# First group of a masked-attention stack on one core: fills, order of keys and queries, mask copies and a fourth buffer for adj

## The chip, the cores and the metric

The kernel runs on one core of a Trainium2 chip. The metric is the device time in microseconds (us). The engines are TensorE (PE), VectorE (DVE), ScalarE (ACT), GpSimd (POOL) and SyncE (SP), which here issues nearly all DMAs, in order, from one queue.

## The reference

`x` has 3327 rows of 256, `adj` is a 3327 x 3327 matrix of 0 and 1. Four layers follow each other, each with a residual and a layer norm; layer 3 holds three attention steps in a row. All use the same `adj` as a mask. The first group, with which this case deals, belongs to layer 0:

```python
def _L0_gnn_ref(features, adj, Wq, Wk):
    Qn = _cos_normalize(features @ Wq.T)      # x / max(|x|, 1e-4)
    Kn = _cos_normalize(features @ Wk.T)
    raw_att = Kn @ Qn.T
    att = softmax(where(adj > 0, raw_att, -9e15), axis=1)
    prop_fea = att @ features
    adj_mask = (sum(adj, axis=1) > 0)[:, None]
    prop_fea = adj_mask * prop_fea + (1.0 - adj_mask) * features
    return 0.5 * prop_fea + 0.5 * features

x = _layernorm(x + _L0_gnn_ref(x, adj, Wq, Wk))     # layer 0
x = _layernorm(x + _L1_gnn_ref(x, adj, W, a))       # layer 1: leaky_relu(s_i + d_j), softmax, elu
x = _layernorm(x + _L2_gnn_ref(x, adj, ...))        # layer 2: q k^T / sqrt(d), softmax, elu
x = _layernorm(x + _L3_gnn_ref(x, adj, ...))        # layer 3: three steps like layer 1
```

## The kernel before

**Tiling.** The rows are padded to 26 tiles of 128 (`NT`). The rows whose result is computed are taken in groups of 512 (`b`, `NB` = 7, the last with 256). A step is one pair of a group `b` and a tile `j` of 128 neighbours: a product `ps` (L493) of 128 neighbours by the 512 rows of the group, an exponential on ScalarE (`ex`, L506), a multiplication with the mask on VectorE (`e`, L507), and four products `po` (L1331, 128x257) with tile `j` of `x`, added up over the 26 steps. The 257th column of `x` is one, so that the sum of the weights comes along. Groups 1 to 5 of layer 0 use other products (L780) and stand outside the change. There are 6 such passes over 7 groups.

**Order.** The main loop makes the weights `e` two to three steps ahead of their `po` (`LA` = 2, function `make`). The program up to step 3 is written out by hand (`tc.manual_schedule`, closed with `start.__exit__` at `s == 3`); after that a planner with its own costs sets the order on each engine, so that moving one instruction can change the order further on. Every engine, and SP's queue too, works its list in order: an instruction that waits holds all behind it.

**The start.** `ones` is set by VectorE; a few products of `ones` with itself (L80) have no use for the result. `count` and `part` are used for the identity matrix `ident` (L94, L96), which later turns tiles on TensorE. Then, for group 0: `queries0(0)` computes the 512 rows of `pk` (L354) in two banks, their squares on ScalarE (L369), the inverse lengths `rk` on VectorE, the scaled rows `kr` (L389 on VectorE, L391 on ScalarE), turns them on TensorE (`pkT`, L395) and copies them to half 1 of `FT[0]` (L396). `keys0(0)` computes the other side turned at once: `pq` (L317), its square (L324), a copy to half 0 of `FT[0]` (L336), the sums of squares `pn` (L330), and from them `qss` and `rq` on VectorE (L338 and the lines 137 to 160). The bank pool `ps_b` has three banks.

**adj.** For each group, `adj` comes in 13 loads of two tiles, 512 KB each (`load_adj`, L425), into tiles with the tag `stage`, of which there are three. `take_adj` makes a byte mask of each; for the first four loads of group 0 that is one `tensor_scalar` (L434), on GpSimd for the first two and on VectorE for the next two; later ones take two passes on ScalarE (L437, L438). `add_adj` adds the two halves into a count (L447, L451); `sum_adj` turns the count (`af`, `pasum`, L462 and L466). A `stage` tile is free again when both have read it. Tiles with other names (`turned`, `p4`, `x4`, `o4`, `x2`) use the same tag in later layers.

**SP's queue at the start:** weights, `xT` of groups 0 and 1, adj (0,0), x tiles 0 to 3, adj (0,2) and (0,4), x tiles 4 to 7, `xT` of group 2, x tile 8, adj (0,6), and so on, with (b, j) for group and first tile.

The order of the parts before the loop is this line:

```python
for part in (k0, q0, k0, q0, q0, k0, q0, k0, q0, q1):
    next(part, None)
```

Of the kernel before, what the change touches and what calls it, by code (L numbers as in the profile page):

```python
# [19 lines left out]
P = 128  # L20
# [13 lines left out]
def gnn_stack(ctx: ExitStack, tc: tile.TileContext, a: dict, N: int, out: bass.AP):  # L34
# [41 lines left out]
    nc.vector.memset(ones, 1.0)  # L76

    turned = bank("turned")
    for _ in range(4):
        nc.tensor.matmul(turned[:, :P], ones, ones, start=True, stop=True)  # L80

    count = const.tile([P, P], F32, name="count")
    n = 8
    for k in range(n):
        nc.vector.memset(count[:, k : k + 1], k + 1.0)
    while n < P:
# [1 line left out]
            count[:, n : 2 * n], count[:, :n], float(n), None, ALU.add  # L88
        )
        n *= 2  # L90
    part = const.tile([P, P], F32, name="part")
    nc.vector.memset(part, 1.0 / (4 * P))
    for k in range(4):
        nc.tensor.matmul(turned[:, :P], count, part, start=(k == 0), stop=(k == 3))  # L94
# [216 lines left out]
    def keys0(g):  # L311

        wd, n = bw(g), len(tiles_of(g))
        xT = xTs[g]
        pm = bank("pq")
        for h in range(2):
            nc.tensor.matmul(  # L317
                pm[:, :wd], w["qk"][:, h, :H], xT[:, h, :wd], start=(h == 0), stop=(h == 1)
            )
            if g == 1 and h == 0:  # L320
                yield
        yield
        sq = work.tile([P, CH], F32, tag="u", name="qsq", bufs=2)
        nc.scalar.activation(sq[:, :wd], pm[:, :wd], AF.Square)  # L324
        if g > 0:
            nc.scalar.copy(FT[g][:, 0, :wd], pm[:, :wd])
        yield
        pn = bank("pn0")
        for k in range(n):
            nc.tensor.matmul(  # L330
                pn[:, k : k + 1], sq[:, k * P : (k + 1) * P], ones[:, :1], start=True, stop=True
            )
        yield
        v = cols.tile([P, 4], F32, tag="qss", name="qss")
        if g == 0:
            nc.scalar.copy(FT[g][:, 0, :wd], pm[:, :wd])  # L336
            yield
            nc.vector.tensor_scalar(v[:, :n], pn[:, :n], COS_EPS * COS_EPS, None, ALU.max)  # L338
            rsqrt(rq[:, 4 * g : 4 * g + n], v[:, :n], n)
        else:  # L340
            nc.scalar.copy(v[:, :n], pn[:, :n])
            lengths(rq[:, 4 * g : 4 * g + n], v[:, :n], n)

    def queries0(g):

        wd, n = bw(g), len(tiles_of(g))
        xT = xTs[g]
        ss = cols.tile([P, 4], F32, tag="kss", name="kss")
        kr = work.tile([P, 4, H], F32, tag="kr", name="kr", bufs=1)
        banks = [bank("pk") for _ in range(2 if g == 0 else 1)]  # L350
        for k in range(n):
            pk = banks[k // 2 if g == 0 else 0][:, k * H : (k + 1) * H]
            for h in range(2):
                nc.tensor.matmul(  # L354
                    pk,
                    xT[:, h, k * P : (k + 1) * P],
                    w["qk"][:, h, H:],
                    start=(h == 0),
                    stop=(h == 1),
                )  # L360
        if g > 0:
            nc.scalar.copy(kr.rearrange("p k n -> p (k n)")[:, :wd], banks[0][:, :wd])
            yield
        src = [
            banks[k // 2][:, k * H : (k + 1) * H] if g == 0 else kr[:, k, :] for k in range(n)
        ]
        for k in range(n):
            jk = work.tile([P, H], F32, tag="sq0", name="sq", bufs=1)
            nc.scalar.activation(jk, src[k], AF.Square, accum_out=ss[:, k : k + 1])  # L369
        yield  # L370
        rk = cols.tile([P, 4], F32, tag="rk", name="rk")
        if g == 0:
            lengths(rk[:, :n], ss[:, :n], n)
        else:
            lengths(rk[:, :n], ss[:, :n], n, nc.gpsimd, "prs")
            for _ in range(4 if g == 1 else 7):
                yield

            r2 = cols.tile([P, 4], F32, tag="rk2", name="rk2")
            nc.vector.scalar_tensor_tensor(  # L380
                r2[:, :n], gate[0][:, :n], 0.0, rk[:, :n], ALU.is_ge, ALU.mult
            )
            rk = r2
        yield
        for k in range(n):
            if g > 0 and k == 2:
                yield
            if g == 0 and k >= 2:
                nc.vector.tensor_scalar(kr[:, k, :], src[k], rk[:, k : k + 1], None, ALU.mult)  # L389
            else:  # L390
                nc.scalar.mul(kr[:, k, :], src[k], rk[:, k : k + 1])  # L391
        yield
        pt = bank("pkT")
        for k in range(n):
            nc.tensor.transpose(pt[:, k * P : (k + 1) * P], kr[:, k, :], ident)  # L395
        nc.scalar.copy(FT[g][:, 1, :wd], pt[:, :wd])  # L396
# [20 lines left out]
    def load_adj():  # L417

        if not adj_order:
            return  # L420
        b, j = adj_order.popleft()
        wd = bw(b)
        st = work.tile([P, 2 * CH], I32, tag="stage", name="stage", bufs=3)
        src = a["adj_a"][b] if wd == CH else a["adj_z"]
        nc.sync.dma_start(st[:, : 2 * wd], src[:, j * wd : (j + 2) * wd])  # L425
        stages[b, j] = st

    def take_adj(b, j):

        wd = bw(b)  # L430
        st = stages[b, j][:, : 2 * wd]
        if b == 0 and j < 8:
            eng = nc.gpsimd if j < 4 else nc.vector
            eng.tensor_scalar(mask(b, j, 2), st, 0, None, ALU.is_gt)  # L434
        else:
            t_ = work.tile([P, 2 * CH], BF16, tag="a", name="pos", bufs=3)
            nc.scalar.activation(t_[:, : 2 * wd], st, AF.Relu)  # L437
            nc.scalar.activation(mask(b, j, 2), t_[:, : 2 * wd], AF.Sign)  # L438
# [45 lines left out]
    def weights0(b, j):  # L484
        wd = bw(b)
        if j % 2 == 0:
            take_adj(b, j)
            load_adj()
        soon = (b, j) in ((0, 0), (0, 2))
        if j % 2 == 0 and not soon:  # L490
            add_adj(b, j)
        ps = bank("ps")
        nc.tensor.matmul(  # L493
            ps[:, :wd],
            FT[j // 4][:, 0, (j % 4) * P : (j % 4 + 1) * P],
            FT[b][:, 1, :wd],
            start=True,
            stop=True,
        )
        t_ = work.tile([P, CH], F32, tag="a", name="ex", bufs=3)  # L500
        e = work.tile([P, CH], F32, tag="e", name="e", bufs=5)

        n = 2 if (b, j) == (0, 0) else 1
        for h in range(n):
            c = slice(h * wd // n, (h + 1) * wd // n)
            nc.scalar.activation(t_[:, c], ps[:, c], AF.Exp, scale=rq[:, j : j + 1])  # L506
            nc.vector.scalar_tensor_tensor(  # L507
                e[:, c], t_[:, c], 0.0, mask(b, j)[:, c], ALU.add, ALU.mult
            )
        if soon:  # L510
            add_adj(b, j)
        return e
# [315 lines left out]
    def turn(x4, n, out, steps=3):  # L828

        half = "p k (n t) -> p t k n"
        pl = work.tile([P, 4, 2, D], U16, tag="x4k", name="planes", bufs=2)
        for t in range(2):
            nc.scalar.copy(pl[:, :n, t, :], x4[:, :n, :].bitcast(U16).rearrange(half, t=2)[:, t])
        yield
        tr = work.tile([P, 16, P], U16, tag="stage", name="turned", bufs=3)
        nc.sync.dma_start_transpose(
            out=tr[:, : 4 * n, :], in_=pl[:, :n].rearrange("p k t n -> p (k t n)")
        )  # L840
        for _ in range(steps):
            yield
        trv = tr[:, : 4 * n, :].rearrange("p (k t h) i -> p t k h i", t=2, h=2)
        for t in range(2):
            nc.vector.tensor_copy(out(t), trv[:, t])  # L845
        yield
# [19 lines left out]
    def finish(L, b, pos):  # L866
# [74 lines left out]
                if k % 2:  # L941
                    yield
        else:
            p4 = work.tile([P, 4, D], F32, tag="stage", name="p4", bufs=3)
            if L.key == "2":
                z = joined(pos, b, p4)
                nc.vector.tensor_scalar(z, z, TINY, None, ALU.max)
# [9 lines left out]
                    nc.vector.reciprocal(ri, ri)  # L957
                    nc.scalar.mul(p4[:, k, :], pos[k][:, :D], ri)  # L958
            if L.key in x_d:
                x4 = work.tile([P, 4, D], F32, tag="stage", name="x4", bufs=3)  # L960
                xr = [x4[:, k, :] for k in range(4)]
                for k, t in enumerate(ts_):
                    nc.sync.dma_start(xr[k], x_d[L.key][t])
            else:
                xr = [cur[t][:, :D] for t in ts_]
# [67 lines left out]
        if not L.hidden:  # L1033
# [3 lines left out]
            rsqrt(r[:, :n], v[:, :n], n)  # L1037
            yield
            if L.key in ("1", "3c"):
                o4 = work.tile([P, 4, D], F32, tag="stage", name="o4", bufs=3)  # L1040
                dsts = [o4[:, k, :] for k in range(n)]
            else:
                dsts = [nxt[t][:, :D] for t in ts_]
# [72 lines left out]

    def fetch_last():

        x2 = work.tile([P, 2, D], F32, tag="stage", name="x2", bufs=3)
        for k, t in enumerate(tiles_of(NB - 1)):  # L1120
            nc.sync.dma_start(x2[:, k, :], x_d["3c"][t])
        xm = work.tile([P, 2, D], F32, tag="acc", name="xm", bufs=2)
# [121 lines left out]
    load_adj()  # L1244
    load_x(0)
    load_adj()
    masks[0] = new_mask(0)
    k0, q0, q1 = queries0(0), keys0(0), keys0(1)
    for part in (k0, q0, k0, q0, q0, k0, q0, k0, q0, q1):
        next(part, None)  # L1250
    make(0)
    next(q1)
# [202 lines left out]
```

## Time and profile before

| | |
|---|---|
| median of 3 runs | 2375.55 us (2374.44 to 2375.63) |
| profiled execution | 2374.08 us |
| its span, first to last instruction | 2372.3 us |
| TensorE busy | 2346.0 us, 99% |
| VectorE busy | 1598.1 us, 67% |
| ScalarE busy | 1223.5 us, 52% |
| GpSimd busy | 43.5 us, 2% |
| mean granted TensorE clock | 0.997 |
| moved by DMA | 214.66 MB |

Times in the timeline count from the first instruction. A busy row of TensorE is no proof of work at its peak, since the ends of products are modelled; the granted clock (1.00 is full) is given apart. The DMA share is the mean busy share of the 16 DMA engines. In the lists of waits a line says which engine waited at which line for whom, the total in us, how often, and the longest. In the timeline an idle time before an instruction and what ended it stand in brackets.

### The profile page before, as it was taken

How to read it: one execution, taken by the hardware profiler on the slowest of the kernel's cores; microseconds unless marked ns; L12 is line 12 of the kernel's file. 1: busy time of each engine (PE TensorE's matmuls, PEld its weight loads, DVE VectorE, ACT ScalarE, POOL GpSimd, SP SyncE). 2: the span in 40 equal slices, each digit the busy share in tenths (PEclk: the TensorE clock that was granted, in tenths of full speed). 3: DMA queues.
4: the chain of work that ended last, by engine and by line, in shares of the span. 5: the costliest groups of instructions: out<-in, count | busy, mean ns of one | idle time of the engine just before them, and what ended most of it. 6: DMA issues, size and time to landing. Idle time of an engine off the chain costs nothing.

```text
span 2372.3 us, 33071 instructions
## 1 busy us (share of the span) xinstructions
PE 2346.0 (99%) x11957; PEld 1914.3 (81%) x11957; DVE 1598.1 (67%) x4243; ACT 1223.5 (52%) x1959; POOL 43.5 (2%) x158
## 2 busy tenths in 40 slices
PE   9999999999999999999999999999999999999997
PEld 6788887888888777667667798888888888888886
DVE  6789999866666657567567585556656555655665
ACT  4667777765555422222222255555655555655554
POOL 1000001000000000000000000000000000000000
PEclk9999999999999999999999999999999999999999
DMA  7555555423232322212212221211211111122120
GB/s 256 188 182 181 185 187 191 161 83 83 74 87 53 105 56 87 78 53 88 74 49 73 80 87 48 75 52 26 76 47 43 43 59 51 44 98 69 61 66 23
DMA packets 147288, 214.66 MB, mean 90 GB/s; under 512 B 76093, under 2 KB 101172, under 8 KB 142516
## 3 DMA queue, kind: packets, MB, share of 16 engines
q1 hardware_dynamic: 146852, 212.28, 29.0%
q8 instruction: 94, 1.54, 0.3%
q14 instruction: 70, 0.57, 0.1%
q10 hardware_dynamic: 272, 0.26, 0.0%
HBM read 167.53 MB, written 28.19 MB: 83 GB/s over the span
## 4 chain that ended last, share of the span: by engine, by line
PE 89%; DVE 5%; DMA 3%; ACT 2%; issue 1%; POOL 0%; SPq 0%; DVEq 0%; ACTq 0%
PE po L1331 47%; PE po L780 18%; PE ps L564 12%; PE ps L493 4%; PE pproj L989 3%; DMA stage<-in_adj_a 1%; PE pv L1075 1%; DMA turned<-planes 1%; DVE e L507 1%; PE pgq L523 1%; PE po L1316 1%; DVE acc L451 1%; ACT re L658 1%; DVE ejunk L592 0%; DVE v L669 0%
## 5 line engine op out<-in xcount | busy, mean ns | idle before, releaser
L1331 PE MATMUL po<-v,e 128*128 128x257 f32 x5616 | 1251.9, 381 | 2.1 <-ACT p L958 1.4
L1331 PEld LDWEIGHTS po<-v,e 128*128 128x128 f32 x5616 | 1062.0, 190 | 169.5 <-ACT p L958 9.4
L658 ACT ACTIVATE re<-u,nrh,th 128x512 f32<-128x512 f32 (+1 forms) x728 | 555.4, 780 | 476.9 <-DVE e L669 472.5
L669 DVE SCALAR_TENSOR_TENSOR e<-re,rh,mask 128x512 f32<-128x512 f32 (+1 forms) x702 | 501.2, 719 | 377.1 <-PE po L1331 348.8
L564 PE MATMUL ps<-gT,ft 128*128 128x512 f32 (+1 forms) x728 | 307.4, 563 | 0.0
L572 ACT ACTIVATE ex<-ps,off 128x512 f32<-128x512 f32 (+1 forms) x182 | 119.1, 656 | 356.8 <-PE ps L564 356.1
L780 PE MATMUL po<-tsums,ssum 128*128 128x128 f32 (+1 forms) x1794 | 250.1, 275 | 0.4 <-DVE ssum L730 0.3
L479 DVE SCALAR_TENSOR_TENSOR e<-ex,mask 128x512 f32<-128x512 f32 (+1 forms) x182 | 118.4, 651 | 162.8 <-ACT ex L572 161.9
L780 PEld LDWEIGHTS po<-tsums,ssum 128*128 128x128 f32 x1794 | 224.7, 192 | 1.7 <-DVE ssum L730 1.0
L564 PEld LDWEIGHTS ps<-gT,ft 128*128 128x128 f32 x728 | 132.1, 190 | 114.5 <-issue 111.7
L780 PEld LDWEIGHTS po<-v,e 128*128 128x128 f32 x1196 | 169.4, 191 | 67.4 <-issue 54.5
L780 PE MATMUL po<-v,e 128*128 128x129 f32 x1196 | 182.6, 275 | 0.0
L506 ACT ACTIVATE ex<-ps,rq 128x512 f32<-128x512 f32 (+1 forms) x183 | 119.1, 652 | 117.9 <-PE ps L493 107.9
L493 PE MATMUL ps<-ft,ft 128*128 128x512 f32 (+1 forms) x312 | 142.5, 561 | 0.0
L507 DVE SCALAR_TENSOR_TENSOR e<-ex,mask 128x512 f32<-128x512 f32 (+1 forms) x183 | 117.1, 647 | 31.6 <-ACT ex L506 27.3
L451 DVE CUSTOM_DVE_ANT_0 acc<-acc,stage 128x1024 uint16<-128x1024 uint16 (+1 forms) x168 | 108.4, 645 | 18.3 <-DMA stage<-in_adj_a 13.9
L780 PE MATMUL po<-tsums,e 128*128 128x128 f32 x598 | 92.3, 275 | 0.1
L780 PE MATMUL po<-v,ssum 128*128 128x128 f32 x598 | 92.3, 275 | 0.0
L438 ACT ACTIVATE mask<-pos 128x1024 uint8<-128x1024 bf16 (+1 forms) x87 | 86.4, 993 | 2.2
L437 ACT ACTIVATE pos<-stage 128x1024 bf16<-128x1024 int32 (+1 forms) x87 | 85.6, 984 | 1.2 <-DVE e L507 1.2
L989 PE MATMUL pproj<-w_l_w,pT 128*128 128x256 f32 x304 | 78.3, 380 | 2.8 <-DVE pT L845 2.7
L780 PEld LDWEIGHTS po<-tsums,e 128*128 128x128 f32 x598 | 79.3, 192 | 0.3 <-issue 0.3
(256 smaller groups left out, 1803.1 us busy)
## 6 DMA issues: line engine op xcount, KB each, us to landing
mask<-mask_d SPq DMA_DIRECT2D x30, 1664.0 KB
stage<-in_adj_a SPq DMA_DIRECT2D x78, 512.0 KB
tsums<-t_d SPq DMA_DIRECT2D x152, 256.5 KB
mask_d<-mask SPq DMA_DIRECT2D x6, 1664.0 KB
u<-s_d SPq DMA_DIRECT2D x24, 256.0 KB
xT<-in_xT SPq DMA_DIRECT2D x10, 512.0 KB
mask<-mask_d SPq DMA_DIRECT2D x5, 832.0 KB
t_d<-tsums SPq DMA_DIRECT2D x14, 256.5 KB
```

The lines of the kernel that those rows point to most:

```text
L451: nc.vector.tensor_tensor(acc, acc, st[:, h * wd : (h + 1) * wd], ALU.add)
L479: nc.vector.scalar_tensor_tensor(e[:, :wd], t_[:, :wd], 0.0, mask(b, j), ALU.add, ALU.mult)
L493: nc.tensor.matmul(ps[:, :wd], FT[j // 4][:, 0, (j % 4) * P : (j % 4 + 1) * P], FT[b][:, 1, :wd], start=True, stop=True,)
L506: nc.scalar.activation(t_[:, c], ps[:, c], AF.Exp, scale=rq[:, j : j + 1])
L507: nc.vector.scalar_tensor_tensor(e[:, c], t_[:, c], 0.0, mask(b, j)[:, c], ALU.add, ALU.mult)
L564: nc.tensor.matmul(ps[:, :wd], FT[j // 4][:, h, (j % 4) * P : (j % 4 + 1) * P], g[:, h, :wd], start=(h == 0), stop=(h == 1),)
L572: nc.scalar.activation(t_[:, :wd], ps[:, :wd], AF.Exp, bias=off, scale=1.0 / D**0.5)
L658: nc.scalar.activation(t_[:, :wd], self.u[b][:, :wd], AF.Relu, bias=self.nrh[:, j : j + 1], scale=self.th[:, j : j + 1],)
L669: nc.vector.scalar_tensor_tensor(e[:, :wd], t_[:, :wd], self.rh[:, j : j + 1], mask(b, j), ALU.add, ALU.mult,)
L780: nc.tensor.matmul(o, x, y, start=(p == 0 and g not in banks[:i]), stop=(p == NT // 2 - 1 and g not in banks[i + 1 :]),)
L989: nc.tensor.matmul(pm[:, :D], pT[:, h, :], w[L.w][:, h, :], start=(h == 0), stop=(h == 1),)
L1331: nc.tensor.matmul(pos[k], es[:, k * P : (k + 1) * P], V[L.i % 2][j], start=(j == 0), stop=(j == NT - 1),)
```

## The change

It touches the start of layer 0 and the number of `stage` tiles.

- Six instead of four products of `ones` (L80).
- `count`, `part` and the scaled rows `kr` get no tiles of their own: the first two use tiles of the tag `ejunk`, `kr` is half 1 of `FT[g]`, where the turned rows are written later.
- For group 0, the copy of `pq` to `FT[0]` comes right behind its square, ahead of the scaled rows on ScalarE; VectorE scales rows 1 to 3 instead of 2 and 3.
- The mask of the first four loads is made by VectorE; that of (0,0) is put in `keys0(0)`, ahead of `qss`.
- A third load of adj is issued ahead of x tiles 4 to 7 (so the one behind it, issued in step 0, is the fourth), and the tag `stage` has four tiles.

```diff
-    for _ in range(4):
+    for _ in range(6):
         nc.tensor.matmul(turned[:, :P], ones, ones, start=True, stop=True)
 
-    count = const.tile([P, P], F32, name="count")
+    count = work.tile([P, D], F32, tag="ejunk", name="count", bufs=2)[:, :P]
...
-    part = const.tile([P, P], F32, name="part")
+    part = work.tile([P, D], F32, tag="ejunk", name="part", bufs=2)[:, :P]
...
         nc.scalar.activation(sq[:, :wd], pm[:, :wd], AF.Square)
-        if g > 0:
-            nc.scalar.copy(FT[g][:, 0, :wd], pm[:, :wd])
+        nc.scalar.copy(FT[g][:, 0, :wd], pm[:, :wd])
...
         if g == 0:
-            nc.scalar.copy(FT[g][:, 0, :wd], pm[:, :wd])
-            yield
+            take_adj(0, 0)
             nc.vector.tensor_scalar(v[:, :n], pn[:, :n], COS_EPS * COS_EPS, None, ALU.max)
...
-        kr = work.tile([P, 4, H], F32, tag="kr", name="kr", bufs=1)
+
+        kr = FT[g][:, 1, :].rearrange("p (k h) -> p k h", h=H)
...
-            nc.scalar.copy(kr.rearrange("p k n -> p (k n)")[:, :wd], banks[0][:, :wd])
+            nc.scalar.copy(FT[g][:, 1, :wd], banks[0][:, :wd])
...
-            if g == 0 and k >= 2:
+            if g == 0 and k > 0:
                 nc.vector.tensor_scalar(kr[:, k, :], src[k], rk[:, k : k + 1], None, ALU.mult)
...
-        st = work.tile([P, 2 * CH], I32, tag="stage", name="stage", bufs=3)
+        st = work.tile([P, 2 * CH], I32, tag="stage", name="stage", bufs=4)
...
         if b == 0 and j < 8:
-            eng = nc.gpsimd if j < 4 else nc.vector
-            eng.tensor_scalar(mask(b, j, 2), st, 0, None, ALU.is_gt)
+            nc.vector.tensor_scalar(mask(b, j, 2), st, 0, None, ALU.is_gt)
...
         if j % 2 == 0:
-            take_adj(b, j)
+            if (b, j) != (0, 0):
+                take_adj(b, j)
             load_adj()
...
     load_adj()
     load_x(0)
     load_adj()
+    load_adj()
     masks[0] = new_mask(0)
     k0, q0, q1 = queries0(0), keys0(0), keys0(1)
-    for part in (k0, q0, k0, q0, q0, k0, q0, k0, q0, q1):
+    for part in (k0, q0, k0, q0, q0, k0, k0, q0, q1):
         next(part, None)
```

The tiles `turned`, `p4`, `x4`, `o4` and `x2` of the tag `stage` get `bufs=4` likewise.

## The prediction

> **What bounds the kernel now.** I read the page first (busy shares), then TensorE's waits over the span and over the first 105 us, then the timeline and one-microsecond windows of the first 24 us.
>
> ```profile
> PE 2346.0 (99%) x11957; PEld 1914.3 (81%) x11957; DVE 1598.1 (67%) x4243; ACT 1223.5 (52%) x1959; POOL 43.5 (2%) x158
> ```
>
> TensorE is busy for 2346.0 of 2372.3 us, so only its 26.3 us of idle time, and time at a low clock, can be won by moving work that it waits for. The timeline of TensorE has no hole from 19.27 (first `po`) to 82.6 us, and after 99.09 none that this change touches. What is in reach lies before 19.27 and in two holes of the first group. Waits of TensorE, then of SP's queue, first 105 us (total, times, longest):
>
> ```profile
> PE pasum L466 <- DVE af L462: 2.1, 1, 2.1
> PE pn L330 <- ACT kr L391: 1.6, 1, 1.6
> ...
> PE pn L330 <- ACT ft L326: 0.6, 1, 0.6
> PE turned L94 <- DVE part L92: 0.6, 1, 0.6
> ...
> SPq L425 <- DVE acc L447: 9.4, 1, 9.4
> ```
>
> The order of the start is in the timeline (start us, length, engine, line):
>
> ```profile
> 1.05 2.08 PE L80 MATMUL turned<-ones 128*128 128x128 f32 x8 [1.05 <-DVE ones L76]
> 3.70 2.08 PE L94 MATMUL turned<-part,count 128*128 128x128 f32 x8 [0.57 <-DVE part L92]
> ...
> 11.39 1.05 PE L330 MATMUL pn<-ones,qsq 128*128 128x1 f32 x8 [1.65 <-ACT kr L391]
> ...
> 13.85 1.91 PE L493 MATMUL ps<-ft 128*128 128x512 f32 x2
> ...
> 15.10 5.56 POOL L434 TENSOR_SCALAR mask<-stage 128x1024 uint8<-128x1024 int32 x2 [12.07 <-issue]
> ...
> 17.95 1.60 DVE L507 SCALAR_TENSOR_TENSOR e<-ex,mask 128x256 f32<-128x256 f32 x2 [3.72 <-POOL mask L434]
> ...
> 19.27 2.00 PE L1331 MATMUL po<-v,e 128*128 128x257 f32 x8 [0.31 <-DVE e L507]
> ```
>
> Two things end at the first `po`: GpSimd's mask (15.10 + 2.82 = 17.92, then `e`), and TensorE's own row of four 512-wide products (ps, pq, ps, ps), which ends at 17.08 + 1.88 - 0.16 = 18.80. The windows say why that row is slow (us, five busy times with counts, granted clock, DMA share, GB/s):
>
> ```profile
> 12.00:13.00 1.00, 1.00 (x9) 1.00 (x10) 0.48 (x4) 0.02 (x1) 0.00 (x0) 1.00 1.11 367
> 13.00:14.00 1.00, 1.00 (x3) 0.39 (x2) 0.83 (x6) 0.56 (x1) 0.00 (x0) 0.73 1.05 384
> 14.00:15.00 1.00, 1.00 (x3) 0.48 (x2) 0.19 (x2) 0.00 (x0) 0.00 (x0) 0.50 0.47 162
> 15.00:16.00 1.00, 1.00 (x2) 0.38 (x2) 0.00 (x0) 0.20 (x1) 0.90 (x1) 0.50 0.00 1
> 16.00:17.00 1.00, 1.00 (x2) 0.34 (x1) 0.00 (x0) 0.64 (x2) 1.00 (x1) 0.56 0.00 0
> 17.00:18.00 1.00, 1.00 (x4) 0.44 (x3) 0.05 (x1) 0.00 (x0) 1.00 (x2) 1.00 0.00 0
> ```
>
> The granted clock is a half from about 13.46 (0.73 over that slice) to 16.88 (0.56), and DMA stands still from 15 to 21: SP's next load of adj waits 9.4 us for a buffer.
>
> **The change, part by part.**
>
> *Fills.* `ones` products start 0.21 us apart (four of two records lie in 2.08 with a tail of 0.37). Six end issuing at 1.05 + 12 x 0.2135 = 3.61; `part` is there at 3.65 and L94 starts at 3.70. Cost nothing, hidden by the 0.57 wait; if the memsets came earlier they would cost 0.43 each. Gain: only through the clock, below.
>
> *Order of keys and queries.* The changed program's list of instructions, each with its waits, shows `ft` (pq) copied on ScalarE before the turned rows; `pn` now waits for that copy alone. ScalarE: square at 9.79, copy 0.48 later (the pitch of L324 to L326), done 10.86; `pn` at 10.9 instead of 11.39. Row 0 follows on ScalarE at 10.75 to 11.11; VectorE's row 1 reads the same bank and is made to wait for it, so rows 1 to 3 (0.35 each, 0.27 apart, as L389) run 11.15 to 12.04. The last turn ends at about 12.36 (12.94 now), ScalarE's copy to `ft` at 12.99 (13.57). ps of step 0 can start behind pq at 13.15, not 13.85: 0.7 us earlier. Rows in their final place (`ft` for `kr`) add no instruction; the later groups only rename. Freed are `kr`, `count`, `part`.
>
> *Mask.* Two GpSimd copies (2.78 each) go, VectorE gets two of 0.69 (the row of L434 there). The one for pair (0,0) stands between row 3 and `qss`: 11.96 to 12.65, so `rq` ends at 12.56 + 1.74 = 14.30 (14.22 now) - 0.08 later, hidden behind ps. Its data: the chain has that load landed at 8.43. The copy for (0,2) stands behind `e` of step 1, in VectorE's slack. VectorE's copy for (0,6) now stands ahead of the first `e`; it waits for the fourth load, and `e` and with it `po` queue behind. That load takes the place in the queue of today's v4 to v7: with it 15 x 256 KB = 3.93 MB have been asked for (1 of w, 2 + 2 of xT, 2 of the first pair, 2 of v0 to v3, 6 of three more pairs), which the summed GB/s column passes at 12.7; with the 1.2 us from bytes to landing of the first load (1.83 MB passed at 7.2, landed 8.43), 13.9. VectorE gets there at 14.3. Margin 0.4; each us beyond 15 costs one. Also gone is the slow first `e`: 1.27 us beside GpSimd's second copy against 0.41 for the other half.
>
> *A rule and a row.* GPSIMD Engine Reference, section 2.1, gives about 6 us for the code of a freshly loaded kernel. Here the configuration is at 3.0 and the first copy at 15.10 with its data there at 8.43: 12 us. By the rule both copies would be over at 9.0 + 5.56 = 14.6, before the first `ex` (15.80), and taking them off GpSimd would be worth nothing; by the row it takes away the 17.92. I take the row. GpSimd's next work is past 60 us, so the loading is then hidden.
>
> *When does `po` start?* Four products of 0.86 = 3.44 us at full clock from 13.15. If the clock halves from 13.46 to 16.88 again: 0.31 done by then, 1.71 during, 1.42 left: 18.3. If it does not: 16.6. `e` is ready in both (15.7; 15.3). TensorE: Matmul & The Clock Gate, "Why this matters for your kernels", says that gaps up to about 3 us do not lower the clock. The longest gap here is 1.65, and it was lowered, so the row decides: the rule would have the change at 16.6. Counted back in steps of the 3.41 us that the low clock lasted, the windows show full clock kept after a stretch with 87% of TensorE busy (6.64 to 10.05) and lost after one with 61% (10.05 to 13.46). With `pn` at 10.9 the latter becomes about 72%: between the two, nearer to 61. I take 18.3, a gain of 0.97, and keep 16.6 (2.67) for the range. Six fills raise the first 3.4 us from 61 to 64%: probably too little to bring the full clock earlier.
>
> *Fourth buffer.* Load (0,6) is issued with the first ones; v4 to v7, xT2 and v8 come 1.4 us later (0.52 MB at 0.385), landing by about 16.5: v4 is used at 33, xT2 at 25, so nothing. The next load waits for the first sum, done about 16.6 instead of 20.15, so the 6 us DMA hole shrinks to little, and all later loads run some 3.5 us ahead, TensorE only 1. The xT3 load is now queued behind the load of (0,10), which waits for the sum of (0,2); it is needed at 35, and that sum ends near 21. What this is worth is read from the two holes only: 0.58 at 82.8 (late VectorE, which had sat 4.3 us behind a load), and 2.06 at 97:
>
> ```profile
> 96.59 1.42 DVE L451 CUSTOM_DVE_ANT_0 acc<-acc,stage 128x1024 uint16<-128x1024 uint16 x2 [1.57 <-DMA stage<-in_adj_a]
> ...
> 99.09 0.63 PE L466 MATMUL pasum<-ident,af 128*128 128x128 f32 x4 [2.06 <-DVE af L462]
> ```
>
> There a sum of the next group (pair (1,4)) stands ahead of `e` and `af`. In the changed order the sum there is that of (1,6), one pair further on, and its load waits for the same mask of (0,24) and stands behind the same store of `tsums`: the buffer is eaten up by the order. `pasum` only stands one product (0.43) later. Bounds: 2.64 if loads are in time, 0 if all is as now, below nothing in the rival. I take 1.2: the first hole and a third of the second.
>
> Later stages: the waits left behind 105 us (3.7 for `pT`, 1.4 for `p`) are on ScalarE, VectorE and the turning DMA, not on that buffer: 0.
>
> Sum against the profiled execution (2374.08, span 2372.3 and 1.8 around it): 0.97 + 1.2 = 2.2, 2371.9. It lies 1.5 below the median of the runs, 2375.55; same step: 2373.3.
>
> **Rivals.**
> *The clock stays up.* 2.67 + 1.2 = 3.9: 2371.7. For it: 72% against 61, the longest gap about 1.3 instead of 1.65, and the rule. Against: no row shows the limit between 61 and 87%.
> *It also rises one window (3.4 us) earlier,* because six fills leave no gap. L94 and the eight `pk` then run at full speed: 0.93 + 0.5 saved, of which the load of xT (0.79 MB, passed at 4.6, landing perhaps 1 us later) leaves some 1.2, an estimate: 5.1 in all, 2370.4. Against: 61 to 64% is little.
> *Slower: a sum ahead of its load.* VectorE works in order; the sum of (1,6) stands ahead of the `e` of the last step and `af`. The hole of 2.06 exists since (1,4) was late there. Should (1,6) come when (1,6) comes now, two steps (5.2 us, `po` starts 2.6 apart) later, the hole is 7.3, and with the start's gain 2375.55 - 1.0 + 5.2 = 2379.8; two such pairs, 2385. It decides once that load lands over 1 us later against TensorE than (1,4) does. Against: one buffer more lets it go a pair earlier.
> *Nothing comes of it:* `po` bound by the (0,6) copy or a new wait: 2375.5.
>
> **How the numbers follow.** 0.2% is 4.75 us, about what a measurement of this kernel can tell from no change. Clock drops again: 0.48, 2373.3 (own range 2371.5 to 2374.8). Clock stays: 0.28, 2371.7, a third of it beyond 0.2% with the holes closed (2.67 + 2.64). Rises earlier: 0.11, counted as faster. Nothing: 0.06. Slower: 0.07, five in seven beyond 0.2%. Faster 0.20, same 0.75, slower 0.05. Range 2369.8 to 2376.4: it leaves out the upper end of the slow case and gains above 5.7.
>
> **What would show it.** First `po` at 18.3 (16.6: clock stayed); granted clock in 13 to 17; `pn` near 10.9; no GpSimd work at 15; first `e` 0.4 long; DMA not at zero between 15 and 21; `pasum` waiting 1 to 2 us; holes near 80. A first `po` after 19, a `pasum` hole over 3 us, or a first `e` behind DMA would prove the steps wrong, and so would a gain after 105 us.

## The result, and the profile after

| | before | after |
|---|---|---|
| median | 2375.49 us (20 runs, 2372.61 to 2378.07) | 2369.95 us (20 runs, 2368.71 to 2372.37) |
| profiled execution | 2374.08 us | 2369.43 us |
| its span | 2372.3 us | 2367.6 us |

The ratio is 0.9978, with a 95% interval of 0.9971 to 0.9985: 5.5 us by the medians, 4.65 us by the two profiled executions. The interval lies wholly below 1, so there is a gain; whether it passes the 0.2% that the forecast takes as its margin, the interval leaves open. The median lies 3.4 us below the forecast time and only 0.15 us inside the lower end of the forecast range, and the gain is 5.5 us where 2.2 were taken. That it fell inside the range was luck: the case held most likely, half clock once more, did not come.

Busy times on the page of the changed kernel:

```profile
PE 2343.5 (99%) x11961; PEld 1914.2 (81%) x11961; DVE 1598.5 (68%) x4246; ACT 1222.4 (52%) x1958; POOL 39.9 (2%) x156
```

TensorE is busy 2.5 us less with four records more. Most of that is the clock: the 3.41 us at half clock, which the windows below no longer have, cost 1.7 us of work. The timeline of the start (start us, length, engine, line; in brackets the idle time before and what ended it):

```profile
1.05 2.93 PE L80 MATMUL turned<-ones 128*128 128x128 f32 x12 [1.05 <-DVE ones L76]
...
11.02 1.05 PE L329 MATMUL pn<-ones,qsq 128*128 128x1 f32 x8 [1.16 <-ACT ft L325]
...
13.30 1.12 PE L492 MATMUL ps<-ft 128*128 128x512 f32 x2
...
14.31 0.69 DVE L432 TENSOR_SCALAR mask<-stage 128x1024 uint8<-128x1024 int32 x1
...
14.99 0.79 DVE L506 SCALAR_TENSOR_TENSOR e<-ex,mask 128x256 f32<-128x256 f32 x2
...
16.84 1.90 PE L1331 MATMUL po<-v,e 128*128 128x257 f32 x8
```

`pn` starts 0.37 us earlier, the first `ps` 0.55, the first `po` 2.43. The two halves of the first `e` take 0.79 together, against 1.60. The windows show where most of the 2.43 is from (us, five busy times with counts, granted clock, DMA share, GB/s):

```profile
13.00:14.00 1.00, 1.00 (x4) 0.46 (x3) 0.86 (x7) 0.25 (x1) 0.00 (x0) 1.00 1.10 366
14.00:15.00 1.00, 1.00 (x3) 0.41 (x3) 0.94 (x4) 0.51 (x2) 0.00 (x0) 1.00 1.07 379
15.00:16.00 1.00, 1.00 (x4) 0.40 (x3) 1.00 (x3) 0.33 (x1) 0.00 (x0) 1.00 0.84 299
16.00:17.00 1.00, 1.00 (x4) 0.52 (x3) 0.48 (x2) 0.69 (x1) 0.00 (x0) 1.00 0.11 39
```

The clock is full where it was a half, GpSimd does nothing, and DMA stands still for about one microsecond instead of five. What is left of the two holes is the wait at the sum of adj, and SP's wait for the first buffer has gone from 9.4 to 3.6:

```profile
94.96 0.63 PE L464 MATMUL pasum<-ident,af 128*128 128x128 f32 x4 [0.88 <-DVE af L460]
```

```profile
SPq L424 <- DVE acc L445: 3.6, 1, 3.6
```

Matching TensorE's products of the two traces in order gives the lead of the changed kernel: 2.43 at the first `po` and 2.53 from the next ones to 75 us, 3.38 behind the place of the hole near 82.8 (now closed), 4.56 behind `pasum`. Then it grows, with two losses (0.6 near 310 us, 0.4 near 630) and gains of 0.2 to 1.0, up to 7.07 at 2050 us, and from there 1.2 and 1.2 are given back, at 2090 and 2290 us: 4.66 at the end. That the start and the two holes add up to nearly the whole is therefore partly chance.

### The profile page after: what moved, and what is told of

The parts are those of the page before. It is cut to its first block, busy times and chain, and to the rows that moved or that the text cites. A ratio compares the mean times of both kernels' runs of the same rounds, so it can differ in the third digit from the quotient of the medians.

```text
span 2367.6 us, 33122 instructions
## 1 busy us (share of the span) xinstructions
PE 2343.5 (99%) x11961; PEld 1914.2 (81%) x11961; DVE 1598.5 (68%) x4246; ACT 1222.4 (52%) x1958; POOL 39.9 (2%) x156
## 4 chain that ended last, share of the span: by engine, by line
PE 96%; DVE 2%; DMA 1%; ACT 1%; issue 0%; SPq 0%; POOL 0%; DVEq 0%; ACTq 0%
PE po L1331 50%; PE po L779 20%; PE ps L563 12%; PE ps L492 6%; PE pproj L988 4%; PE pv L1074 1%; PE pgq L522 1%; PE po L1316 1%; PE pk L353 1%; DMA stage<-in_adj_a 0%; PE pq L317 0%; DVE v L668 0%; DVE e L506 0%; DVE acc L449 0%; PE pn L329 0%
```

## The experiments

Each ratio is to the kernel before, measured on the same chip (95% interval); its medians there were 2374.63 us (e1 to e4), 2374.21 (e5 to e8) and 2374.97 (e9 to e12), so that medians of different rows are better compared by their ratios. "First po" and the rest are from the one profiled execution of each kernel.

| run | median us | ratio | first po | half clock, us | wait at pasum |
|---|---|---|---|---|---|
| before | | 1 | 19.27 | 13.46 to 16.88 | 2.06 |
| after | 2369.95 | 0.9978 | 16.84 | none | 0.88 |
| e9_changed_again | 2370.12 | 0.9982 (0.9976 to 0.9989) | 16.76 | none | 1.36 |
| e1_four_fills | 2370.99 | 0.9984 (0.9976 to 0.9991) | 16.77 | none | 3.10 |
| e2_three_buffers | 2372.05 | 0.9988 (0.9981 to 0.9994) | 16.71 | none | 2.36 |
| e3_gpsimd_masks | 2372.00 | 0.9990 (0.9983 to 0.9996) | 19.00 | 10.71 to 14.12 | 1.10 |
| e4_old_order | 2371.93 | 0.9987 (0.9981 to 0.9994) | 18.21 | 12.30 to 15.71 | 1.71 |
| e5_bridge | 2365.87 | 0.9965 (0.9952 to 0.9977) | 15.65 | none | 1.12 |
| e6_sum_earlier | 2370.10 | 0.9982 (0.9975 to 0.9989) | 17.02 | none | none |
| e7_masks_alone | 2373.75 | 0.9997 (0.9989 to 1.0006) | 18.80 | 13.48 to 16.89, 98.81 to 102.23 | 2.53 |
| e8_bridge_before | 2373.58 | 0.9996 (0.9988 to 1.0005) | 17.84 | none | 2.10 |
| e10_bridge_three | 2369.09 | 0.9976 (0.9968 to 0.9984) | 16.71 | 98.77 to 102.18 | 2.90 |
| e11_bridge_stores | 2368.34 | 0.9975 (0.9965 to 0.9984) | 16.57 | none | 1.15 |
| e12_before_both | 2372.22 | 0.9990 (0.9982 to 0.9998) | 17.91 | 96.99 to 100.40 | 2.31 |

(The half clock after TensorE's last products, in every run, is left out.)

### One part undone

```diff
-    for _ in range(6):
+    for _ in range(4):
         nc.tensor.matmul(turned[:, :P], ones, ones, start=True, stop=True)
```

> The changed kernel with four fills in place of six; all else as changed. Own theory (the fills end before the operands of the next products are there, and the clock is kept by the shorter idle stretch before pn): first po product at 16.8 us as in the changed kernel, clock full from 7 to 20 us, time 2370.0 (within 0.7 of the changed kernel). Rival (the two more fills keep the clock): half clock for about 3.4 us somewhere in 12 to 17 us, first po product near 18.3, time 2371.5 or more.

The clock is full from 6.73 us on and the first `po` comes at 16.77: two fills more or less do not keep the clock. The median, 2370.99, is 1.0 above the changed kernel's, where 0.7 was allowed; the intervals of the two ratios overlap. But the wait at `pasum` is 3.10 instead of 0.88. The edit changed the planner's order on VectorE and SP further on, and this shows what the wait really is:

```profile
87.05 2.67 SPq L713 DMA_DIRECT2D t_d<-tsums  x2
89.81 0.38 SPq L424 DMA_DIRECT2D stage<-in_adj_a  x1
```

```profile
94.61 1.42 DVE L449 CUSTOM_DVE_ANT_0 acc<-acc,stage 128x1024 uint16<-128x1024 uint16 x2 [2.92 <-DMA stage<-in_adj_a]
...
96.55 0.42 DVE L460 CAST af<-acc 128x512 f32<-128x512 int32 x1
```

```profile
97.11 0.63 PE L464 MATMUL pasum<-ident,af 128*128 128x128 f32 x4 [3.10 <-DVE af L460]
```

VectorE and SP work through their lists in order, as these rows show: in the changed kernel the last adds of group 0 are over at 67 us, yet `af`, which copies that sum, starts at 94.39. It stands on VectorE behind the two adds of load (1,6), of the next group, and these wait for the load's landing. SP issues the load behind two stores of `tsums` (88.11 in the changed kernel, 89.81 here), and it lands 4.3 to 4.8 us later.

The second kernel puts three buffers and two early loads back (`bufs=3` for the tag `stage` everywhere):

```diff
     load_adj()
     load_x(0)
     load_adj()
-    load_adj()
```

> The changed kernel with three buffers for entries of adj and without the third load before the loop; all else as changed. Own theory (the start gains 2.5 us by the order and the masks, the fourth buffer closes the later holes): first po product at 16.8, the hole at about 80 us and a pasum wait of about 2 us are back, time 2371.5 to 2372.3. Rival (the earlier start alone closes the holes, the buffer is worth nothing): pasum wait near 0.9, no hole at 80 us, time 2370.0.

Start as in the changed kernel, wait at `pasum` 2.36, and the hole near 80 us did not come back: the own theory is half right. The time, 2372.05, is as it had it, though this hole stayed closed. With e1 beside it (four buffers, 3.10) the number of buffers alone does not set the wait.

```diff
-            nc.vector.tensor_scalar(mask(b, j, 2), st, 0, None, ALU.is_gt)
+            eng = nc.gpsimd if j < 4 else nc.vector
+            eng.tensor_scalar(mask(b, j, 2), st, 0, None, ALU.is_gt)
```

> The changed kernel with the first two masks again by GpSimd; all else as changed. Own theory (GpSimd's masks bound the start): mask(0,0) ends at 17.9, the first e takes 1.2 us beside the second mask, first po product at 19.2 although the clock stays full, time 2372.4 (2.4 over the changed kernel). Rival (the clock was the bound, masks come free): first po product by 17.3, time 2370.0 to 2370.6.

First `po` at 19.00, behind `e`, as expected. Not expected was the clock: TensorE's idle stretch ahead of `pn` is the same 1.16 us as in the changed kernel, and here it cost half a clock. Timeline and windows of e3:

```profile
9.63 1.05 PE L329 MATMUL pn<-ones,qsq 128*128 128x1 f32 x8 [1.16 <-ACT ft L325]
...
19.00 1.42 PE L1332 MATMUL po<-v,e 128*128 128x257 f32 x5 [1.84 <-DVE e L507]
```

```profile
10.00:11.00 1.00, 1.00 (x10) 1.00 (x10) 0.96 (x6) 0.00 (x0) 0.00 (x0) 0.85 1.04 418
11.00:12.00 1.00, 1.00 (x4) 0.64 (x3) 0.86 (x7) 0.40 (x1) 0.00 (x0) 0.50 1.02 410
```

The trace's record of the granted clock suggests why. In all traces here it changes at moments that are whole multiples of 3.413 us apart. In e3 one such window runs from 7.30 to 10.71 and holds the whole idle stretch (8.47 to 9.63); the next window has half clock. In the changed kernel the bound between two windows, 10.28, falls into the stretch: 0.42 us of it lies in one window, 0.74 in the other, and neither lowers the clock. GpSimd's masks, the one edit, begin only at 14.83, after the clock fell. One execution of each does not prove it; e4 and the bridged kernels below change the idle stretch itself.

```diff
-        nc.scalar.copy(FT[g][:, 0, :wd], pm[:, :wd])
+        if g > 0:
+            nc.scalar.copy(FT[g][:, 0, :wd], pm[:, :wd])
...
         if g == 0:
+            nc.scalar.copy(FT[g][:, 0, :wd], pm[:, :wd])
+            yield
             take_adj(0, 0)
...
-            if g == 0 and k > 0:
+            if g == 0 and k >= 2:
...
-    for part in (k0, q0, k0, q0, q0, k0, k0, q0, q1):
+    for part in (k0, q0, k0, q0, q0, k0, q0, k0, q0, q1):
```

> The changed kernel with the old order of keys and queries: the copy of turned keys behind the scaled rows, two of these rows on ACT; masks on VectorE and four buffers stay. Own theory (the copy put ahead lets pn start 0.4 us earlier, and that keeps the clock): pn at 11.4 after an idle stretch of 1.6 us, half clock for 3.4 us from about 13.5, first po product at about 18.3, time 2371.5. Rival (the order is worth nothing, the masks are all of the start's gain): full clock, first po product at 16.8 to 17.2, time 2370.0 to 2370.4.

As the own theory had it: idle 1.65, half clock from 12.30 to 15.71, first `po` at 18.21.

```profile
10.84 1.05 PE L330 MATMUL pn<-ones,qsq 128*128 128x1 f32 x8 [1.65 <-ACT ft L393]
```

### Bridging the idle stretch

```diff
+        if g == 0:
+            fill = ps_o.tile([P, D + 1], F32, tag="po", name="fill")
+            for _ in range(4):
+                nc.tensor.matmul(fill[:, :P], ones, ones, start=True, stop=True)
         yield
         sq = work.tile([P, CH], F32, tag="u", name="qsq", bufs=2)
```

> The changed kernel with four more products of ones (into a bank of their own, read by nobody) between the products of the turned keys and pn, in the stretch in which TensorE waits 1.2 us. Own theory (the clock is granted in windows of 3.4 us; a window with more than about 1 us without a product is followed by one at half clock, so the changed kernel keeps its clock in some executions and loses it in others, by where the windows fall): full clock from 7 to 20 us, first po product at 16.8 or a little before, time 2369.0, one below the changed kernel's 2370.0, and the runs lie closer together. Rival (the changed kernel keeps its clock in every execution): nothing to gain, 2370.0, or later by up to 0.3 where the added products delay pn.

2365.87, its five runs between 2365.32 and 2366.60; the lowest of 39 runs of the changed kernel (two sessions, other chips) is 2368.71. The gain is 4.1 us by the medians and 3.1 by the ratios, with intervals that just overlap, where 1.0 was expected. On its own chip the five runs lie below all 17 of e6 (2369.41 to 2370.84), whose time is that of the changed kernel. Five runs are too few to tell whether they lie closer together.

```profile
8.51 1.05 PE L325 MATMUL fill<-ones 128*128 128x128 f32 x8
9.84 1.05 PE L333 MATMUL pn<-ones,qsq 128*128 128x1 f32 x8 [0.27 <-ACT ft L329]
...
15.65 1.90 PE L1335 MATMUL po<-v,e 128*128 128x257 f32 x8
```

In this execution the clock rose at 4.10 us, one window early, which made TensorE 1.19 us earlier than in the changed kernel; e3 had risen at 3.88, was 1.39 earlier at 9 us, and lost 1.55 at the next window. e5, with 0.27 us of idle time left ahead of `pn`, kept the clock. The other 2.8 us of its lead over the changed kernel in the profile have nothing to do with the start: 0.25 is lost at `pasum`, 0.9 won near 310 us, and 0.85 and 1.2 at the two late waits, which are smaller here. So this execution had an early rise besides, and more than half of its lead is no effect of the clock; the changed kernel kept its clock in both its profiles, so that what the bridge saves it at the start is not shown by them.

In the kernel before, six such products (`range(6)`) fill most of its 1.65 us (0.31 is left):

> The kernel before with six more products of ones (into a bank of their own, read by nobody) in TensorE's idle stretch of 1.6 us ahead of pn; masks, order and buffers as before. Own theory (GpSimd's mask ends at 17.9 whatever the clock): clock full from 7 to 20 us, TensorE waits about 1.5 us more for the first e, first po product at 19.2, time as before, within 0.5. Rival (the half clock was the bound): first po product at 17.6, time 1.7 below before.

The clock stayed full, but GpSimd began its first mask at 13.68 in this execution, 1.4 us earlier than in the profile of before, so that the first `po` could come at 17.84, waiting 0.35 for `e`:

```profile
13.68 5.56 POOL L438 TENSOR_SCALAR mask<-stage 128x1024 uint8<-128x1024 int32 x2 [10.65 <-DMA v<-in_x]
...
17.84 2.00 PE L1335 MATMUL po<-v,e 128*128 128x257 f32 x8 [0.35 <-DVE e L511]
```

The run cannot decide between the two bounds; by the medians no gain is shown (0.9996). The other bound alone, the masks on VectorE in the kernel before:

```diff
-            eng = nc.gpsimd if j < 4 else nc.vector
-            eng.tensor_scalar(mask(b, j, 2), st, 0, None, ALU.is_gt)
+            nc.vector.tensor_scalar(mask(b, j, 2), st, 0, None, ALU.is_gt)
```

> The kernel before with one part of the change: the first two masks by VectorE. Own theory (with the masks early, the half clock after the idle stretch of 1.6 us is the bound that is left): half clock for 3.4 us within 12 to 17 us, first po product at 18.0 to 18.4 in place of 19.3, time 2374.5 (1.0 below before). Rival (the masks are all of the start's gain): first po product at 16.9, time 2373.1 (2.4 below).

First `po` at 18.80, half clock before it:

```profile
18.80 1.90 PE L1330 MATMUL po<-v,e 128*128 128x257 f32 x8
```

That is half a microsecond at the start, less than the expected 0.9 to 1.3, and no gain is shown in the end (0.9997). In the profiled execution, the slowest of its runs, `pasum` waited 2.53 us and half clock followed there too. Both edits together:

> The kernel before with the six bridging products and the first two masks by VectorE: the two bounds of the start taken away together, old order, three buffers. Own theory (each alone leaves the other bound): full clock from 7 us, first po product at 16.9 to 17.3 in place of 19.3, a wait at pasum of 2 to 3 us, time 2371.5 to 2372.3, some 2.5 below before. Rival (the new order is what the start needs): first po product at 18 or later, time 2373.5.

```profile
17.91 1.90 PE L1334 MATMUL po<-v,e 128*128 128x257 f32 x8
```

As measured this misses the expected 16.9 to 17.3 and is near the rival's 18. But the clock rose late here, at 8.24, which put TensorE 0.76 behind the profile of before up to 12 us; 17.15 without that is an estimate, and in the expected stretch. The median, 2372.22, is as expected (rival 2373.5) and next to the 2372.05 of e2, which has the new order and three buffers as well. So masks and clock bound the start together, and the rival that the new order is needed beyond its effect on the idle stretch is not borne out.

All five profiles with the bridge (e5, e8, e10, e11, e12) kept the clock at the start, and all three with the old order and no bridge (before, e4, e7) lost it. In time the bridge goes with 0.13% (e5 against after), 0.12 (e10 against e2), 0.07 (e12 against e7) and 0.04 (e8 against before); how much of that is the clock and how much the moved late waits is not separated.

### The wait at pasum

```diff
-        if L.key == "0" and j == NT - 1 - LA:
+        if L.key == "0" and j == NT - 2 - LA:
             sum_adj(b)
```

> The changed kernel with the turn of the first block's sum of adj (af, pasum) handed out one step earlier, which puts af ahead of the adds of the next block's fourth entry on VectorE. Own theory (the wait of 0.9 us at pasum is no wait for the sum, which is whole at 67 us, but for the landing of that entry at 92.4, whose adds stand before af): no wait at pasum, time 2369.1, 0.9 below the changed kernel. Rival (TensorE meets another wait in its place, or the time is given back at a later wait): pasum's wait gone or moved, time 2370.0.

The edit moves the sum in every group of layer 0, not in the first alone. `af` now stands ahead of the adds of (1,6), at 90.08 against 92.60, and the wait is gone:

```profile
90.65 0.63 PE L464 MATMUL pasum<-ident,af 128*128 128x128 f32 x4
```

So what `pasum` waited for is shown: the landing of another group's load. The time did not move (2370.10), as the rival had it. Against the changed kernel this execution goes from 0.18 behind to 0.85 ahead at the hole, loses about 0.3 at the end of each of groups 1 to 4, 0.7 in group 5, where `pasum` now waits 0.49, and 0.5 in the last, and wins 0.9 near 310 us; at 500 us it is 0.67 behind. Handing the sum out earlier in group 0 alone was not tried.

e10 is the bridged kernel with the edit of e2, e11 the bridged kernel with this one:

```diff
-        nc.sync.dma_start(t_d[key][p], t)
+        (nc.gpsimd if key == "0" else nc.sync).dma_start(t_d[key][p], t)
```

> The changed kernel with the four bridging products and with three buffers for entries of adj and no third load before the loop. Own theory (the fourth buffer is worth what the wait at pasum grows without it, as 0.9 grew to 2.4 in the run with three buffers): start as in the bridged kernel, wait at pasum 2.4 to 2.7, time 2367.3, 1.4 over the bridged kernel. Rival (the wait is given back at later waits): 2365.9 to 2366.3.

> The changed kernel with the four bridging products and with the stores of the first layer's sums of rows (t_d) issued by GpSimd in place of SP. Own theory (the load whose landing pasum waits for stands on SP behind these stores, which wait for VectorE's sums): that load is issued some us earlier, no wait at pasum, time 2364.9, 1.0 below the bridged kernel. Rival (the wait moves, or GpSimd's own issue of the stores holds something): 2365.9 or more.

e10 waits 2.90 at `pasum`, and then half clock follows (windows of e10):

```profile
97.60 0.63 PE L468 MATMUL pasum<-ident,af 128*128 128x128 f32 x4 [2.90 <-DVE af L464]
```

```profile
98.00:100.00 2.00, 2.00 (x8) 1.20 (x6) 1.03 (x3) 0.69 (x1) 0.00 (x0) 0.69 0.94 388
100.00:102.00 2.00, 2.00 (x6) 1.61 (x5) 1.12 (x2) 0.00 (x0) 0.00 (x0) 0.50 0.38 154
```

In that execution e10 loses 4.6 us to e5 between 20 and 100 us, and the hole near 80 us, closed in e2, is back (0.46 at 81.01); it is the slowest of its runs. By the medians it is 3.2 (1.4 was expected), on different chips, with intervals that overlap. e11 is a miss: the load is issued at 89.49, later than in e5 (86.93), because with the stores gone SP waits for ScalarE to release the buffer; `pasum` waits 1.15, and a new wait of 1.30 at the `pn` of a later group appears. Stores and buffers hold the same load.

### The changed kernel once more

> The changed kernel once more, nothing edited: a second profiled execution of the same program, on another chip. Own theory (the clock's windows of 3.4 us fall differently in each execution, and the start and the late waits follow): median 2370.0 as before; the profile shows the clock rise at another time than 6.9 us, and where one window takes in more than about 1.1 us of the idle stretch ahead of pn, half clock for 3.4 us and the first po product at 18.0 to 18.3 in place of 16.8. The two late waits of 1.2 us before pproj (at about 2090 and 2290 us) are there again if they belong to the program, and differ if they belong to the execution. Rival (clock and start belong to the program): full clock from 6.9 us, first po product at 16.8 again.

The windows fell nearly as before (rise at 6.71), with the first `po` at 16.76: this execution did not show the other case, and that the changed kernel itself ever loses the clock at the start is not shown. The wait at `pasum` was 1.36 instead of 0.88 for the same program, and the span 0.9 longer. The two late waits came again; the whole-span waits of this kind, in the changed kernel and in e1:

```profile
PE pproj L988 <- DVE pT L844: 5.3, 6, 1.4
```

```profile
PE pproj L988 <- DVE pT L844: 3.9, 6, 1.4
```

They go with the program: at both places the turning DMA, mostly 4.3 us from issue to the copy behind it, takes 5.9 to 6.1 in all traces with six products of ones ahead of `po` (after, e2, e3, e4, e6, e9), 4.3 to 4.6 in before, e1 and e7 (four of them), 4.7 to 5.2 in e5, e8, e10, e11 and e12 (ten). So the time goes with the number of instructions that TensorE has ahead of that place. What may link the two is the loading of instructions. Over the 14 traces there are 252 such transfers of 4 us or more behind 1400 us. During 50 of them a packet of instructions (16 KB, about 0.95 us) is loaded, and these took 4.3 to 6.1 us; of the other 202, all but six took under 4.4 and none over 4.75. Every one over 4.75 has such a packet, then, and its place moves with the number of instructions. Some quick ones have one too (4.34 in before), so why it delays one transfer by 1.7 us and another hardly at all stays open.

## Why the prediction was right or wrong

- *Bounds of the start.* Right: GpSimd's mask (e3: 19.00) and the half clock (e4: 18.21) each bound the first `po`, and taking away one leaves the other (e7: 18.80).
- *Fills cost nothing, and do little to the clock.* Nearly right for their own time (L94 at 3.77 in place of 3.70). Whether they help the clock is open: it rose early in three of nine traces with six fills (3.88, 4.10, 5.47) and in none of five with four (6.64 to 8.24). What was left out: they shift the planner's order (`pasum` 3.10 with four, 0.88 with six) and the late waits.
- *Order.* `pn` 11.02 for 10.9, `ps` 13.30 for 13.15, mask of (0,0) 12.06 for 11.96. Right.
- *A rule and a row.* The row held: in e3 GpSimd began its first mask at 14.83. The rule was misread. GPSIMD Engine Reference, section 2.1, in the Trainium skill takes the wait for the event out of its 6 us, so they are not to be counted from the configuration at 3.05. Counted from the landing of the load (8.43, 8.17, 8.53), the first mask began after 6.67 us in before, 6.66 in e3 and 5.15 in e8: rule and row agree, and by both it pays to take the masks off GpSimd. That the loading of code fills this time is shown by no run.
- *Load (0,6).* Landed 14.14 for 13.9; VectorE came at 14.31 for 14.3. The margin was 0.17 instead of 0.4, and it held.
- *When does `po` start?* This step failed. 18.3 was taken, 16.84 came, near the 16.6 kept for the range: the term 0.97 is 2.43. The reasoning took the low clock to follow from a busy share between 61 and 87% (by the rows the 87 is 91: TensorE idles 0.30 of 3.41 us there), and placed the windows as in the one trace of before. The windows lie elsewhere in each execution: the idle stretch of 1.16 us kept the clock in after, e1, e2, e6 and e9, where a bound between windows cut it in two, and lost it in e3, where one window held it all. The Trainium skill, TensorE: Matmul & The Clock Gate, section "What's actually happening", says that the window of 3413 ns runs freely and does not start with the kernel; the 3.413 us between clock changes here agree. That section should have been weighed beside the one on gaps of 3 us, whose limit these traces do not bear out (1.16 to 1.65 us were enough). By it, the right form of this term is a chance of two values, not one value.
- *Fourth buffer.* 1.2 was taken; the two holes gave 0.85 and 1.18, 2.03 together, not all of it surely by the buffer, since with three the first stayed closed in e2 and came back in e10. The warning that the adds of (1,6) stand ahead of `af` was the right mechanism (e1, e6), but "the buffer is eaten up by the order" was too strong: the load was issued 4.2 us earlier than the load that before waits for (88.11 for 92.30). The size of the wait is no property of the buffer: 0.88 and 1.36 in two executions of one program, 3.10 after an edit elsewhere.
- *Later stages 0.* Right in the sum, wrong in the parts: up to 2.5 more was won after 105 us, and 2.4 given back at the late waits.
- *Rival "the clock stays up", with the holes closed:* 2.67 + 2.64 was the bound given; 2.43 + 2.03 came. This is the case that the profile shows.
- *Rival "it also rises one window earlier":* not in the two profiles of the changed kernel (6.87, 6.71), but in e3 and e5, whose first products are the same (3.88, 4.10). There it put TensorE 1.39 and 1.19 us ahead, as the estimate of 1.2 had it.
- *Rival "a sum ahead of its load":* there as a mechanism, but 0.88 us in size where 7.3 was feared.

## What to carry to other kernels

Where one engine's idle stretch costs clock, count its idle time per window of the clock, in several executions: a stretch of the same length may be free in one and cost 1.55 us in the next (e3), and a few products that nobody reads, put into the stretch, kept the clock in all five profiles that had them. Do not put the whole gain down to that: of the 4.0 us by which e5's profile leads the changed kernel's, 1.2 are an early rise of the clock and 2.8 waits elsewhere. Read a wait through to its end before giving it a cause: `pasum` seemed to wait for its sum, and waited for a load of another group that stood ahead of it in two queues. In a program whose order a planner sets, an edit at the start is also an edit of everything behind it, so look at the late waits before calling a small gain the edit's own.

## What was not expected of the hardware

- In the 14 traces the first half clock after work had begun follows a window with 1.16 us (e3), 1.34 (e7), 1.35 (before) and 1.65 (e4) without products, and at the later hole half clock follows 2.17 (e7, e12) and 2.24 (e10). Idle time alone does not set these apart: windows with 1.46 (e3, from 17.54 us), 1.77 (before, from 95.38) and 1.83 (e2, from 91.93) kept the clock. The early windows also hold the one-column products `pn`. If these are counted as no work up to the next product (0.92 us), the clock was kept with up to 1.83 and lost from 2.08 of 3.41 us. That is a reading of these traces, not tried by itself, and it does not fit the end of the program, where 1.43 us (e4) were enough.
- GpSimd's first mask began at 15.10, 14.83 and 13.68 us in before, e3 and e8, 5.15 to 6.67 us after its data landed. The profile names a later landing of an x tile as what ended the wait (e8's row above); it counts on the same semaphore as the load, and VectorE took its first mask from that load at 12.06 (after) and 10.68 (e4), ahead of the x tile. So it was not the data, and what GpSimd waited for is not shown.
- A VectorE instruction on 128x4 elements (L145) took 1.11 us in e8, beside the start of GpSimd's mask at 13.68; elsewhere it takes 0.16.
